# Layer 3 attention scores: bf16 penalties issued ahead of the fp32 score products in some steps

## Chip, cores and metric

The kernel runs on one core of a Trainium2 chip. The metric is the device time of one execution in microseconds (us); lower is better. Before the change the median of three runs is 3193.77 us.

## What is computed

The reference applies four layers to a tensor of 4 images, 256 channels, 48 x 48 points. Each layer is `x = x + conv(groupnorm(x))`. Layers 0 to 2 are convolutions. Layer 3, which the change touches, is a linear attention over square windows of three sizes (whole side, half, quarter), eight heads of 32 channels:

```
for w in WINDOWS:                      # 1, 2, 4
    ws = Hh // w
    wk = _box(Ik, ws, Hh, Ww)          # box sums of k over a ws x ws window
    wkv = _box(Ikv, ws, Hh, Ww)        # box sums of k v^T
    attn = jnp.einsum('bdhw,bdfhw->bfhw', q, wkv)
    norm = jnp.einsum('bdhw,bdhw->bhw', q, wk)
    outs.append((attn / (norm[:, None] + 1e-06)).reshape(b, C, Hh, Ww))
o = jnp.concatenate(outs, axis=1)
return jnp.einsum('bchw,oc->bohw', o, Wout) + bout[None, :, None, None]
```

`q` and `k` are sigmoids, so every product of a query with a key is positive.

## The kernel before

Everything runs in one launch. Layers 0 to 2 fill the time up to about 1405 us of the trace; from there to the end layer 3 runs, with the projections of the next image (`proj_ps`) woven in.

Layer 3 doesn't form box sums of `k v^T`. It computes scores, query times key, masks away the keys that a query's window doesn't hold, and multiplies by `v`. The loop goes over 48 blocks: 4 images, 2 groups of four heads (`ct`), 6 bands of eight query rows (`rb`). A block is a list of steps from `steps_of` (L1968). One step makes scores for 128 keys (8 rows by 16 columns) at a time against up to 512 query columns for each of four heads. Each head's scores fill one PSUM bank of 512 fp32; two heads share a tile `s` of two banks, so a step has two tiles, called pair 0 and pair 1 here. The pool `ps_s` holds just these two tiles, so the scores of a step wait until the masking of the step before has read its pair.

There are four kinds of step:

- **near** (`add_half`, L1952): keys of the same band or the next one, two products per head, of 320 and 192 columns, and all three windows. Penalties cover columns 192 to 384, so they cut through both products.
- **packed** (`add_strips`, L1930): keys two bands away. Three products of 128 columns each hold the columns that the widest window sees in part; penalties cover just these 384 columns. `add_middle` puts one product of 112 or 117 columns of the middle window behind them.
- **far** (`add_far`, L1938): keys three bands away, two halves, products of 280 and 168 columns (keys below) or 320 and 192 (keys above). Penalties cover all 448 or 512 columns.
- **middles**: what of the middle window found no room in a packed step; no penalties.

The widest window is masked by **penalties**: a matmul of `picks` (24 rows of each 32-row group, 128 columns, bf16) with columns of `masks` (bf16) adds -1024 where a key isn't seen, and a ReLU in `masked` (L2039) makes these scores zero. The other two windows are masked by a product with a 0/1 mask on DVE, and on POOL for the smallest.

`scores` (L2012) issues, for each product, pair 0's two heads and pair 1's two heads, each head in its own 32-row group of the array. An fp32 matmul becomes two loads of weights and two passes. After all products come the penalties, in the same order of heads. The first product in the bank has `start=True`; later ones write into columns of the bank not yet written, or, like the penalties, add onto what stands there.

The order on every engine is the program's: `pe`, `dve`, `act`, `pool` and `sync` are wrapped in `InOrder`. The main loop at the end of the kernel issues, for position n of the stream, the scores of step n, its masking, then the sums (`acc`, products with `v`, method `sums`, L2146) of step n-2, and lets `advance` issue other jobs (projections, `keys_ps`, `out_ps`, norms) as far as a planned time allows. In steps with parts of the middle window ACT masks pair 1 first and DVE pair 0, then they change places; in far steps ACT takes pair 0 and DVE pair 1.

On PE the scores use the array as 32-row tiles (shown as 32*128 or 24*128), and the work before and after them uses 32-column tiles (128*32) or 32*32. All matmuls are issued through one helper line, so the profile shows L251 for all of them; groups are told apart by the names of the tiles: `s<-qs,ks` are score products, `s<-masks` penalties.

Of the kernel before, what the change touches and what calls it, by code (L numbers as in the profile page):

```python
# [254 lines left out]
def conv_preact_kernel(  # L255
# [1374 lines left out]
    with (  # L1630
# [371 lines left out]
        class Block:  # L2002
# [8 lines left out]

            def scores(self, st):  # L2012
                ss = [ps_s.tile([P, 2, 512], F32, tag="s", name="s") for _ in range(NPR)]
                for a, c, ranges, (r0, r1), at, n in st.products:
                    for pr, s in enumerate(ss):
                        for j in range(2):
                            head = slice((2 * pr + j) * D, (2 * pr + j + 1) * D)
                            pe.matmul(
                                s[:, j, at : at + n],
                                kvs[self.b, self.ct, a][0][head, c, :],  # L2020
                                of_columns(self.qs[head], ranges, r0, r1),
                                start=(at == 0),
                                stop=not st.penalties and at + n == st.columns,
                            )
                for lo, hi, first in st.penalties:
                    for pr, s in enumerate(ss):
                        for j in range(2):
                            g = 2 * pr + j
                            rows = slice(g * D, g * D + RB + KC)
                            pe.matmul(  # L2030
                                s[:, j, lo:hi],
                                picks[rows, :],
                                masks[rows, PEN_AT + first : PEN_AT + first + hi - lo],
                                start=False,
                                stop=True,
                            )
                return ss

            def masked(self, st, ss):  # L2039

# [128 lines left out]
        def of_columns(t, ranges, r0, r1):  # L2169

            (x0, x1), n = ranges[0], len(ranges)
            if n == 1:
                return t[:, x0:x1, r0:r1]
            size, apart = x1 - x0, ranges[1][0] - x0
            assert n == 2 and x0 == 0 and apart % size == 0 and ranges[1][1] == apart + size
            return t.rearrange("p (g x) r -> p g x r", x=size)[
                :, 0 : apart // size + 1 : apart // size, :, r0:r1
            ]
# [191 lines left out]
        for n in range(len(stream) + LAG):  # L2370
            if n < len(stream):
                i, st, at, last = stream[n]
                if at == 0:
                    begun(i)
                ss = blocks[i].scores(st)
# [3 lines left out]
            if n >= LAG:  # L2379
                i, st, at, last = stream[n - LAG]  # L2380
# [64 lines left out]
```

## Time and profile before

| | |
|---|---|
| runs of the kernel before | 3193.77, 3187.84, 3198.49 us; median 3193.77 |
| the profiled execution | 3194.66 us, of which the span of instructions is 3192.8 us |
| mean granted TensorE clock | 0.955 of full speed; 0.98 from 1420 us to the end |
| layer 3's share of the span | about 1405 to 3192.8 us |
| busy in 1420 to 3192 us (1772 us) | PE 1678.7, DVE 1082.9, POOL 1176.5, ACT 712.9 us |
| score products `s<-qs,ks` | 8704 passes, 589.1 us busy |
| penalties `s<-masks` | 1664 matmuls (416 steps of four), 168.3 us busy |
| idle time of `s<-qs,ks` weight loads | 256.2 us in 8704, of which 77.7 us until ACT has released a pair |

PE's records are pipelined: a matmul's duration holds a fixed latency besides the time in which its columns stream, and neighbours overlap. Distances from start to start are what the work takes; durations compare only with durations of the same kind. PEld are the loads of weights; PE can load the next weights while a matmul streams.

### The profile page before, as it was taken

To read this page: it belongs to the slowest core of one execution; us is meant where nothing else is said; L and a number is where in the kernel's file an instruction comes from. 1 tells how busy PE (TensorE), PEld (TensorE's weight loads), DVE (VectorE), ACT (ScalarE), POOL (GpSimd) and SP (SyncE) were. 2 spreads that over 40 slices of the span, in tenths; PEclk is the share of its full clock that TensorE was granted. 3 is DMA by queue.
4 is the path that set the end of the run, shared out by engine and by line. 5 is a ranking of instruction groups with operands and counts; after the bars stand their busy time and mean duration, and the time that the engine had idled before them with its cause. 6 is when DMAs were issued, how large, how long until landed. Compare 5 with 4: busy or idle time off the path is not lost.

```text
span 3192.8 us, 98649 instructions
## 1 busy us (share of the span) xinstructions
PE 2866.5 (90%) x42698; PEld 2024.3 (63%) x42698; DVE 2002.8 (63%) x3779; ACT 994.5 (31%) x1965; POOL 1356.8 (42%) x1915
## 2 busy tenths in 40 slices
PE   3678999898989987889998899898999989999999
PEld 2456868677766856576665556565666655666665
DVE  7976658747855831376776666675546765555454
ACT  0002211121111144325543235553236532333322
POOL 0000012003000312046788877787757687644443
PEclk9788899999999988899999999999999999999999
DMA  8746512431443144324565765564544456411222
GB/s 276 212 161 185 159 62 103 130 123 53 136 123 110 60 127 146 111 79 140 162 200 147 215 187 156 163 192 142 162 138 144 141 157 186 134 40 44 89 76 69
DMA packets 380037, 434.05 MB, mean 136 GB/s; under 512 B 129843, under 2 KB 335443, under 8 KB 378451
## 3 DMA queue, kind: packets, MB, share of 16 engines
q1 hardware_dynamic: 378403, 425.76, 43.3%
q8 instruction: 338, 5.54, 0.8%
q0 software_dynamic: 144, 1.17, 0.2%
q10 hardware_dynamic: 1056, 0.79, 0.1%
q14 instruction: 96, 0.79, 0.1%
HBM read 288.11 MB, written 140.68 MB: 134 GB/s over the span
## 4 chain that ended last, share of the span: by engine, by line
PE 62%; DVE 11%; POOL 4%; DMA 4%; ACT 3%; issue 2%; SPq 2%; ACTq 0%; DVEq 0%; POOLq 0%
PE s L251 16%; PE cv L251 15%; PE acc L251 15%; PE out_ps L251 5%; PE proj_ps L251 5%; PE ap L251 3%; DVE sm L251 2%; DVE l2v L251 2%; SPq L251 2%; POOL sm L251 2%; POOL nhi L251 1%; ACT sm L251 1%; DVE v L251 1%; PE keys_ps L251 1%; DVE x L251 1%
## 5 line engine op out<-in xcount | busy, mean ns | idle before, releaser
L251 DVE TENSOR_TENSOR sm<-s,masks 128x448 f32<-128x448 f32 (+9 forms) x1408 | 619.9, 497 | 437.1 <-PE s L251 379.5
L251 POOL TENSOR_TENSOR sm<-sm,masks 128x704 f32<-128x704 f32 (+11 forms) x512 | 596.5, 1186 | 513.9 <-DVE sm L251 513.5
L251 ACT ACTIVATE sm<-s 128x384 f32<-128x384 f32 (+2 forms) x736 | 441.5, 609 | 746.6 <-PE s L251 589.7
L251 PE MATMUL cv<-vx,wt 128*128 128x288 f32 x2080 | 562.6, 427 | 92.2 <-DVE vx L251 49.9
L251 PE MATMUL s<-qs,ks 32*128 32x320 f32 (+10 forms) x8704 | 589.1, 360 | 34.7 <-ACT sm L251 20.1
L251 PE MATMUL acc<-sm,vs 128*32 128x128 f32 (+19 forms) x18432 | 606.0, 276 | 6.3 <-issue 6.2
L251 PEld LDWEIGHTS acc<-sm,vs 128*32 128x32 f32 x18432 | 443.0, 110 | 190.2 <-issue 143.4
L251 PEld LDWEIGHTS s<-qs,ks 32*128 32x128 f32 x8704 | 395.1, 186 | 256.2 <-issue 112.0
L251 PEld LDWEIGHTS cv<-vx,wt 128*128 128x128 f32 x2080 | 404.5, 199 | 214.6 <-issue 56.8
L251 POOL MEMSET v<- 128x16 f32 (+1 forms) x120 | 18.7, 216 | 765.0 <-DVE vx L251 639.8
L251 PE MATMUL cv<-v,wl 128*128 128x384 f32 x1152 | 226.8, 357 | 27.3 <-DVE x L251 9.4
L251 PEld LDWEIGHTS cv<-v,wl 128*128 128x128 f32 x1152 | 216.7, 197 | 38.4 <-issue 17.9
L251 DVE TENSOR_SCALAR sm<-s 128x896 f32<-128x896 f32 (+1 forms) x96 | 110.9, 1156 | 116.0 <-PE s L251 92.5
L251 PE MATMUL s<-masks 24*128 24x192 bf16 (+3 forms) x1664 | 168.3, 284 | 0.0
L251 POOL TENSOR_TENSOR v<-l2v,v 128x384 fp32r<-128x384 f32 x96 | 108.5, 1160 | 120.4 <-ACT v L251 111.7
L251 PE MATMUL cv<-pad,wl 128*128 128x384 bf16 x864 | 145.5, 331 | 5.1 <-ACT pad L251 5.1
L251 POOL TENSOR_TENSOR nhi<-nhi,nq 128x384 f32<-128x384 f32 x144 | 147.9, 1047 | 0.0
L251 PE MATMUL out_ps<-o,wout_sb 128*32 128x384 f32 x1152 | 122.0, 495 | 6.2 <-ACT ns L251 2.4
L251 PEld LDWEIGHTS <-wl 128*128 128x128 bf16 x864 | 84.5, 98 | 65.5 <-issue 7.9
L251 PE MATMUL out_ps<-stage,wout_sb 128*32 128x384 f32 x1152 | 121.8, 491 | 0.2 <-issue 0.2
L251 DVE TENSOR_TENSOR pt<-cs 128x184 f32<-128x184 f32 x144 | 120.1, 838 | 0.1
L251 PE MATMUL ap<-seen,xT 120*128 120x120 f32 (+3 forms) x832 | 120.1, 304 | 0.0
(175 smaller groups left out, 3419.8 us busy)
## 6 DMA issues: line engine op xcount, KB each, us to landing
wt<-wt SPq DMA_DIRECT2D x48, 768.0 KB
kb_d<-pt SPq DMA_DIRECT2D x48, 576.0 KB
rc<-r_d SPq DMA_DIRECT2D x192, 144.0 KB
nhi<-kb_d SPq DMA_DIRECT2D x120, 192.0 KB
nlo<-kb_d SPq DMA_DIRECT2D x88, 192.0 KB
o_d<-stage SPq DMA_DIRECT2D x24, 576.0 KB
o<-o_d SPq DMA_DIRECT2D x24, 576.0 KB
wl<-wl_d SPq DMA_DIRECT2D x16, 768.0 KB
```

The source lines that it names most:

```text
L251: return lambda *args, **kwargs: self.tc.keep_in_program_order(op(*args, **kwargs))
```

## The change

In steps in which every product lies either wholly inside the penalties' columns or wholly outside, `scores` now calls the penalties first: they open the bank (`start=True`), and the products are added onto them where they overlap. In the other steps the order stays. The penalties' loop moves into a method of its own, `penalise`. The test `ahead_` is true for packed, far and middles steps and false for near ones; middles have no penalties, so nothing is issued differently there.

```
             def scores(self, st):
                 ss = [ps_s.tile([P, 2, 512], F32, tag="s", name="s") for _ in range(NPR)]
-                for a, c, ranges, (r0, r1), at, n in st.products:
+                ahead_ = all(at + n <= st.lo or at >= st.hi or (st.lo <= at and at + n <= st.hi) for *_, at, n in st.products)
+                if ahead_:
+                    self.penalise(st, ss, True)
+                for m, (a, c, ranges, (r0, r1), at, n) in enumerate(st.products):
                     for pr, s in enumerate(ss):
                         for j in range(2):
...
-                                start=(at == 0),
-                                stop=not st.penalties and at + n == st.columns,
+                                start=m == 0 and not (ahead_ and st.penalties),
+                                stop=(ahead_ or not st.penalties) and m == len(st.products) - 1,
                             )
+                if not ahead_:
+                    self.penalise(st, ss, False)
+                return ss
+
+            def penalise(self, st, ss, opening):
+
                 for lo, hi, first in st.penalties:
                     for pr, s in enumerate(ss):
                         for j in range(2):
...
-                                start=False,
-                                stop=True,
+                                start=opening,
+                                stop=not opening,
                             )
-                return ss
```

The number of matmuls, their shapes and operands, the tiles of the array that they use and everything on the other engines stay as they were.

## The prediction

> **What bounds the kernel now.** I read the page's busy times and its chain of work first. The chain is the work that ended last, followed back.
>
> ```profile
> PE 2866.5 (90%) x42698; PEld 2024.3 (63%) x42698; DVE 2002.8 (63%) x3779; ACT 994.5 (31%) x1965; POOL 1356.8 (42%) x1915
> ...
> PE 62%; DVE 11%; POOL 4%; DMA 4%; ACT 3%; issue 2%; SPq 2%; ACTq 0%; DVEq 0%; POOLq 0%
> ```
>
> PE carries the chain. In layer 3 it does so more: asked for 1530 to 3192 us alone, the chain has PE s 29.4%, acc 26.3%, out_ps 10.0%, proj_ps 6.4%, keys_ps and norm_ps 1.5% each, 75% in all. The masking (DVE, POOL and ACT `sm`, 9.4%) stands between one step's scores and the next. A stretch of the chain in order of time (start us, us, what):
>
> ```profile
> 2474.15 0.86 PE proj_ps L251 x16
> 2475.01 1.16 PE s L251 x20
> 2476.17 1.46 PE acc L251 x48
> 2477.64 0.86 PE proj_ps L251 x16
> 2478.50 1.29 PE s L251 x20
> 2479.79 0.87 PE acc L251 x32
> ```
>
> PE goes from scores to sums to filler without a pause; every ns cut from such a piece of `s` moves what follows.
>
> **Which steps change.** The groups by shape, for 1405 to 3192 us, give the penalties by width (shapes, count, busy us, mean ns):
>
> ```profile
> L251 PE MATMUL s<-masks 24*128 24x192 bf16 x1024 | 88.8, 244 | 0.0
> ...
> L251 PE MATMUL s<-masks 24*128 24x384 bf16 x256 | 29.7, 325 | 0.0
> L251 PE MATMUL s<-masks 24*128 24x512 bf16 x192 | 26.6, 376 | 0.0
> ```
>
> Width 192 is the near steps: strips from column 192 to 384 cut both products, so they stay. 384 wide is packed (256/4 = 64 steps), 512 is far with keys above (48), and the rest of the 1664, 192 matmuls of width 448, is far with keys below (48). **160 of 416 steps change.**
>
> **One far step on PE**, timeline of PE from 2399.2 us (start us, us for the union of the row, xcount):
>
> ```profile
> 2399.00 0.51 PE L251 MATMUL proj_ps<-xn,wq_sb 128*32 128x384 f32 x4
> 2399.44 1.04 PE L251 MATMUL s<-qs,ks 32*128 32x168 f32 x16
> 2400.30 0.37 PE L251 MATMUL s<-masks 24*128 24x448 bf16 x4
> 2400.60 0.82 PE L251 MATMUL acc<-sm,vs 128*32 128x280 f32 x12
> ```
>
> An fp32 pass streams two cycles a column at 2.4 GHz, a bf16 one one cycle: here start-to-start distances are 140 ns for 168 columns, 235 for 280. The last of the four proj_ps passes starts at 2399.02 and streams 320 ns to 2399.34; scores start at 2399.44, a drain of 96 ns. Penalties start at 2400.30, stream 187 ns, the last of the four heads starts 20 ns behind the first, and sums start at 2400.60, a drain of 92 ns. From scores to sums: 1.16 us.
>
> Within it, the durations of the first four score passes and of those that follow (min/median/max):
>
> ```profile
> L251 PE MATMUL s<-qs,ks x4: 405/405/405, 2399.4 to 2399.5; 32*128 32x168 f32 x4
> ...
> L251 PE MATMUL s<-qs,ks x11: 301/394/405, 2399.4 to 2399.8; 32*128 32x168 f32 x7, 32*128 32x280 f32 x4
> ```
>
> A 168-column pass takes 301 ns, the first 405: 104 ns more. Its weights are loaded at that very moment (the loads start at 2399.44 too, so they were not pulled ahead across the drain). Later loads lie behind a streaming pass. **A step opens with one exposed load of fp32 weights.** What a load costs is plain where matmuls stream a single column, at 348 us:
>
> ```profile
> 347.78 1.03 PE L251 MATMUL sum_ps<-ones,wl 128*128 128x1 f32 x8
> ...
> 348.67 0.29 PE L251 MATMUL sum_ps<-ones_b,kept 128*128 128x1 bf16 x6
> ```
>
> With single durations of 250 and 163 ns (groups of that stretch), the distance is (1030-250)/7 = 111 ns for fp32 weights and (290-163)/5 = 25 ns for bf16.
>
> **What the Trainium skill says.** "TensorE: Matmul & The Clock Gate", section "LDWEIGHTS (loading the stationary operand)": a load takes its columns over 1.2 GHz, 107 ns for 128, whatever the rows; the trace agrees (104 exposed, 111 apart). Its section "Weight-path perf modes" says that non-fp32 weights of 128 columns load fast, measured at about twice; the trace has 111 against 25 ns, more than four times, and decides. Penalty loads have this width: they last 95 ns in the record against 186 for the score weights. "TensorEngine Tiling (Array Packing)", section "Key Properties": a change of tiling mode drains the array; the trace has 92 to 96 ns. Penalties and scores are both tiled by 32 rows, so their order changes no mode. "PSUM — Partial Sum Buffer", section "The four PSUM rules": the opening matmul clears the bank's bits, later ones add where something was written and overwrite elsewhere; no time hangs on that in any row here.
>
> **The change, part by part.** *Opening with a bf16 load*: the exposed load falls from 107 to 25 ns, -82 ns. *fp32 weights behind the penalties*: 107 ns of load beside 160, 187 or 213 ns of streaming (384, 448, 512 columns), so nothing; if that cover fails, +107. *Penalties at the end*: gone; their weight loads were hidden behind score passes, so only their stream moves. *Exit*: the drain stays; middles steps already leave from an fp32 pass with the same 92 ns. Sum for the far step: before 107 + 2x140 + 2x233 + 187 + 20 + 92 = 1152 (measured 1160), after 25 + 187 + 746 + 20 + 92 = 1070. For the packed step at 2176.86 (penalties 2177.85, sums 2178.12: 1.26 us) the eight passes go at the load's pace, 111 ns: before 107 + 7x111 + 98 + 160 + 20 + 92 = 1254, after 1172. Both -82.
>
> The switch from bf16 to fp32 in one row group is shown nowhere in this tiling. Nearest is the 128*128 tiling of layer 1, where an fp32 product follows a bf16 one:
>
> ```profile
> 736.41 0.33 PE L251 MATMUL cv<-pad,wl 128*128 128x384 bf16 x1
> 736.58 0.65 PE L251 MATMUL cv<-vx,wt 128*128 128x288 f32 x2
> ```
>
> 0.17 us against 160 ns of streaming: load hidden, no drain. I take 0. Bounds: no gain below this, as there is no less work than none; a loss up to a drain of 96 and a reload of 107.
>
> *Waits*: the wait for a pair's release moves from the first product to the penalty. Behind pair 1's penalty now stand all products of pair 0; before, pair 0's first product ran while pair 1 was awaited. This matters in the steps in which PE stalls inside, some 80 of the 160 by their start-to-sums distances (over 60 ns beyond the shortest). There pair 1's row groups end last and set the exit; their own sequence is shorter by the same 82 ns. Pair 0 led by up to its first product, two passes (214 ns packed, 280 to 533 far), and now leads by a penalty (160 to 213). In the worst case, a stalled far step that opens with its wide product, pair 0 ends 533-213-82 = 240 ns later. Its reader is ACT (896 or 1024 elements, about 1.0 us); DVE, which starts later on pair 1 and takes 1.13 to 1.23 us, ends last. So I take 0, and 20 steps x 0.24 = 5 us as the bound. No queue other than PE's changes; DMAs, masks and the planner's costs stay.
>
> **The sum.** 160 x 82 ns = 13.1 us of PE work, all of it in the chain's kind of piece. It reaches the end only where the chain goes through the step. Followed back in the trace, the chain covers 80% of the changed steps' time on PE (PE's 75% plus some of the masking in series with it says the same); elsewhere POOL, a DMA or the queue sets the pace. So 13.1 x 0.8 = 10.5 us. The profiled execution, 3194.66 us (span 3192.8 and 1.9 around it), lies 0.9 above the median of the runs; off the median, 3193.8 - 10.5 = **3183 us**. Next to bind in a shortened step is the same PE queue.
>
> **Rivals.** *A, the forecast*: 3183; with 65 to 100% landing and the scatter of the runs, 3178 to 3188. *B, the gain is mostly absorbed*: score loads waited 77.7 us for ACT's release, half of the changed steps stall, and a later pair 0 costs up to 5 us; with a third of it left, 4 us, 3190. Against it: the masking waits for the scores far longer (DVE idle 379.5, ACT 589.7 us until PE `s`), so most masking starts sooner too. *C, slower*: in a row group the fp32 weights can't load behind a bf16 pass, or the switch drains. Drain and reload, 96 + 107 - 82 = +121 ns a step, x 160 x 0.8 = 15.5 us: 3209. It decides from 82 ns of extra a step. Against it stand the rows at 736 us, and that at 2184.74 us penalties of one pair stream beside products of the other. *That nothing is reordered* is excluded by the columns of far and packed steps.
>
> **Chances.** A 0.70, B 0.22, C 0.08. About 0.3%, 9.6 us, is what this measurement can tell from no change, and A's centre lies just beyond it: I give A 0.78 to pass it, B 0.05. Faster 0.56, slower 0.06 (C past +9.6), same 0.38. The range 3177 to 3192 holds A and most of B.
>
> **What would show it.** Right: far steps 1.08 and packed 1.17 us from start to sums when unstalled; the first row is `s<-masks`, the first fp32 pass with its ordinary duration; `s<-masks` takes over the idle time ahead of scores. C shows as more than 190 ns from a 448-wide penalty to its product. B shows as shorter steps with longer waits of PE for ACT or DVE. Wrong altogether: if the opening bf16 load in this tiling isn't 25 ns.

## The result, and the profile after

Over six runs the changed kernel takes 3169.37 us in the median (3160.70 to 3179.41), the kernel before 3193.52 (3187.84 to 3198.49). The ratio is **0.9932, 95% interval [0.9912, 0.9952]**: 22 us faster, twice what was forecast, and below the range of 3177 to 3192. Run twice more beside other kernels, it gave 0.9945 [0.9927, 0.9963] and 0.9915 [0.9894, 0.9936]. The profiled execution took 3170.42 us, its span 3168.6.

On the page after, the busy times, the chain of work that ended last, and the groups of the two kinds of matmul:

```profile
PE 2838.8 (90%) x42698; PEld 2009.7 (63%) x42698; DVE 2001.7 (63%) x3779; ACT 993.4 (31%) x1965; POOL 1355.0 (43%) x1915
...
PE 63%; DVE 12%; ACT 4%; POOL 3%; DMA 3%; issue 3%; SPq 1%; DVEq 0%; ACTq 0%; POOLq 0%
...
L251 PE MATMUL s<-qs,ks 32*128 32x320 f32 (+10 forms) x8704 | 551.8, 353 | 24.6 <-ACT sm L251 16.5
...
L251 PE MATMUL s<-masks 24*128 24x192 bf16 (+3 forms) x1664 | 171.6, 287 | 12.8 <-ACT sm L251 8.7
```

The counts are those of before; the other engines' busy times moved by 1 to 2 us. PE still bounds the kernel. `s<-qs,ks` went from 589.1 to 551.8 us busy for the same 8704 passes: not less work, but less time in which a pass waited for its weights. `s<-masks` now has idle time ahead of it, since it comes first.

Split by shape, layer 3 of before (after the bar: busy us, mean ns of one; then idle us ahead):

```profile
L251 PE MATMUL s<-qs,ks 32*128 32x128 f32 x1536 | 77.5, 293 | 9.8 <-ACT sm L251 6.0 <-DMA ks<-k_d 2.3 <-DVE sm L251 0.4
...
L251 PE MATMUL s<-qs,ks 32*128 32x168 f32 x384 | 32.9, 332 | 1.9 <-issue 0.9 <-ACT sm L251 0.8
...
L251 PE MATMUL s<-masks 24*128 24x448 bf16 x192 | 23.2, 349 | 0.0
```

and of after:

```profile
L251 PE MATMUL s<-qs,ks 32*128 32x128 f32 x1536 | 60.0, 277 | 0.1
...
L251 PE MATMUL s<-masks 24*128 24x384 bf16 x256 | 32.8, 333 | 9.8 <-ACT sm L251 7.0 <-DVE sm L251 0.5
...
L251 PE MATMUL s<-qs,ks 32*128 32x168 f32 x384 | 23.7, 303 | 0.0
L251 PE MATMUL s<-masks 24*128 24x448 bf16 x192 | 23.2, 359 | 2.2 <-ACT sm L251 1.0
```

The mean 168-column product falls from 332 to 303 ns, which is the duration of a pass whose load is hidden (301). The 448-wide penalty, 349 ns at the end of a step, takes 359 ns at its start: a mere 10 ns for being first, where the product paid 104. The 9.8 us of idle time ahead of packed steps have changed owner and not size.

**An unstalled far step**, the one that the prediction dissected, timeline of PE after:

```profile
2386.06 0.83 PE L251 MATMUL proj_ps<-xn,wq_sb 128*32 128x384 f32 x8
2386.82 0.37 PE L251 MATMUL s<-masks 24*128 24x448 bf16 x4
2387.02 0.93 PE L251 MATMUL s<-qs,ks 32*128 32x168 f32 x16
2387.88 0.68 PE L251 MATMUL acc<-sm,vs 128*32 128x280 f32 x8
```

From start to sums it is 1.06 us where it was 1.16. The single starts, in ns from the first penalty, are 0 (penalty), 200, 347 (168 columns), 488 and on (280 columns), 1057 (sums). (Where this text says how long a matmul streams, that is an estimate from distances: 140 ns for 168 fp32 columns, here and in the prediction, and half of that for a bf16 column, from the 431 ns that two matmuls of 512 add in the dose below.) Over all unstalled changed steps the median difference is **-104 ns** (far and packed alike).

**A stalled packed step**, one in which pair 1 has to wait for its reader. Timeline of before:

```profile
2412.87 0.61 PE L251 MATMUL proj_ps<-wv_sb,xn 128*32 128x256 f32 x8
2412.95 0.59 DVE L251 TENSOR_TENSOR sm<-s,masks 128x432 f32<-128x432 f32 x1
...
2413.41 1.27 PE L251 MATMUL s<-qs,ks 32*128 32x128 f32 x29
...
2414.93 0.40 PE L251 MATMUL acc<-sm,vs 128*32 128x224 f32 x4
```

and the same step after:

```profile
2400.14 0.61 PE L251 MATMUL proj_ps<-wv_sb,xn 128*32 128x256 f32 x8
2400.22 0.59 DVE L251 TENSOR_TENSOR sm<-s,masks 128x432 f32<-128x432 f32 x1
...
2400.69 0.52 PE L251 MATMUL s<-masks 24*128 24x384 bf16 x4
...
2400.88 1.21 PE L251 MATMUL s<-qs,ks 32*128 32x128 f32 x32
...
2402.02 0.40 PE L251 MATMUL acc<-sm,vs 128*32 128x224 f32 x4
```

Work before it, its reader on DVE and its work are the same; scores to sums go from 1.52 to 1.33 us. Over all stalled changed steps the median is **-185 ns**, 80 more than in the unstalled ones. The single starts show where (ns from the first pass of pair 0; the third kernel is an experiment below):

```
                                        before   after   split wait
DVE ends reading pair 1's old scores       124     124      125
pair 1: row that carries the DVE wait      163     177      178
pair 1: first matmul                       270     181      182
pair 1: first matmul of the product        270     357      190
sums start                                1515    1329     1439
```

In before, the row at 163 stands among the weight loads, but it loads nothing: the trace names it `EVENT_SEMAPHORE`. It is an instruction of its own that waits for DVE and takes 51 ns. Only at 239 does the load of the weights follow, carrying a second wait, and at 270 the first pass. **From the reader's end to pair 1's first matmul it is 146 ns before and 57 ns after.** From there to the sums it is 1245 and 1148, -97. The two make the -186 of this step.

The instructions of the trace say what differs. Before, pair 1's first fp32 product needs two waits, one on DVE (the reader) and one on PE's own counter, and one of them stands in an extra instruction. The penalty's load and its matmul carry one each:

```
before   EVENT_SEMAPHORE      [waits DVE]
         LDWEIGHTS s<-qs,ks   [waits PE]
         MATMUL    s<-qs,ks
after    LDWEIGHTS masks      [waits DVE]
         MATMUL    s<-masks   [waits PE]
```

In layer 3 the extra instructions that wait for DVE fell from 358 to 214. That fp32 as such starts late is excluded by other rows of before. From the semaphore's update to the first pass, where that is under 220 ns, it is 136 ns in the median of 127 fp32 products behind an extra instruction, but 44 ns in the median of 170 fp32 products with a single wait, on ACT; of those with a single wait on DVE, 25 take 40 to 49. Bf16 penalties with one wait on the load and one on the matmul take 47 ns (73 in after). (Counted from the reader's end, each is about 10 ns more.)

In sum, 79 unstalled steps x 104 ns and 80 stalled ones x 185 ns are 8.2 + 14.8 = **23.0 us** of PE work (the first step of all, which waits for layer 2, is left out). Near and middles steps have a median of 0. Layer 3, from its first score matmul to the end, took 1781.1 us before and 1781.0 when run again; after, 1759.8, 1764.4 and 1751.3 in the three profiles, 22.6 less on average. The third lost a little less to the throttle: 32 us of clock in layer 3 (time times the share not granted), against 35 to 36 in the other four.

### The profile page after: what moved, and what is told of

It reads as the page before. It is cut to its first block, busy times and chain, and to the rows that moved or that the text cites. A ratio compares the mean times of both kernels' runs of the same rounds, so it can differ in the third digit from the quotient of the medians.

```text
span 3168.6 us, 98361 instructions
## 1 busy us (share of the span) xinstructions
PE 2838.8 (90%) x42698; PEld 2009.7 (63%) x42698; DVE 2001.7 (63%) x3779; ACT 993.4 (31%) x1965; POOL 1355.0 (43%) x1915
## 4 chain that ended last, share of the span: by engine, by line
PE 63%; DVE 12%; ACT 4%; POOL 3%; DMA 3%; issue 3%; SPq 1%; DVEq 0%; ACTq 0%; POOLq 0%
PE s L251 16%; PE cv L251 15%; PE acc L251 15%; PE out_ps L251 5%; PE proj_ps L251 5%; DVE sm L251 3%; PE ap L251 2%; DVE l2v L251 2%; POOL sm L251 1%; ACT sm L251 1%; DVE v L251 1%; POOL nhi L251 1%; SPq L251 1%; PE keys_ps L251 1%; DVE x L251 1%
## 5 line engine op out<-in xcount | busy, mean ns | idle before, releaser
L251 PE MATMUL s<-qs,ks 32*128 32x320 f32 (+10 forms) x8704 | 551.8, 353 | 24.6 <-ACT sm L251 16.5
L251 PEld LDWEIGHTS s<-qs,ks 32*128 32x128 f32 x8704 | 384.0, 186 | 170.6 <-issue 75.3
L251 PEld LDWEIGHTS <-masks 24*128 24x128 bf16 x1664 | 65.7, 92 | 100.0 <-issue 61.0
```

Of the source, the lines that this page charges most:

```text
L251: return lambda *args, **kwargs: self.tc.keep_in_program_order(op(*args, **kwargs))
```

## The experiments

Two theories stood against each other for the part beyond the forecast. **W**: pair 1's first fp32 product starts late because both waits are on it, and any bf16 matmul ahead of it that takes one of them over mends this. **L**: all of it comes from the opening load, and stalled steps merely show it twice, once for each pair. All ratios are to the kernel before, on the same chip.

**The split wait alone.** The order stays that of before. In the 160 steps a bf16 matmul of one column goes ahead of pair 1's first product, which writes over it:

```
+    def touch(self, s, pr, j, n):
+        g = 2 * pr + j
+        rows = slice(g * D, g * D + RB + KC)
+        pe.matmul(s[:, j, 0:n], picks[rows, :], masks[rows, PEN_AT : PEN_AT + n],
+                  start=True, stop=True)
...
+    if m == 0 and pr == 1 and j == 0 and (far or packed):
+        self.touch(s, pr, j, 1)
     pe.matmul(s[:, j, at : at + n], ...)
```

> The order of before (products, then penalties). In far and packed steps one bf16 matmul of a single column, whose value the product behind it overwrites, is put ahead of pair 1's first product, so that the two waits of that product are split over its load and its pass. Theory W (an fp32 product that waits for two semaphores starts 146 ns after the reader of its bank ends, a bf16 load and pass with one wait each 57 ns after): pair 1 starts some 89 ns sooner in the 80 stalled steps, unstalled steps lose 0 to 10 ns, so 5 to 7 us less than before, about 3187. Theory L (all of the gain is the opening load and its cover): nothing gained, 3193 to 3195.

Measured 0.9944 [0.9924, 0.9964]; again:

> The first experiment once more, because its 0.9944 of before is more than its own steps show (80 stalled steps 76 ns shorter, unstalled ones 14 ns longer: 5 us, 9 us with what else moved in that trace). If the step times tell all: 4 to 9 us less than before, 0.997 to 0.999. If splitting the wait does something more that the steps do not show: 0.994 again, as far below before as the changed kernel of the same call.

0.9938 [0.9920, 0.9955]. The stalled step from above:

```profile
2402.34 0.59 DVE L251 TENSOR_TENSOR sm<-s,masks 128x432 f32<-128x432 f32 x1
...
2402.81 0.38 PE L251 MATMUL s<-qs,ks 32*128 32x128 f32 x2
2402.99 0.17 PE L251 MATMUL s<-masks 24*128 24x1 bf16 x1
...
2403.00 1.04 PE L251 MATMUL s<-qs,ks 32*128 32x128 f32 x28
...
2404.25 0.59 PE L251 MATMUL acc<-sm,vs 128*32 128x224 f32 x8
```

Pair 1's product now starts beside the one-column matmul, 65 ns after the reader's end where it was 146. Stalled steps are 77 ns shorter in the median, unstalled ones 14 longer (the extra matmul). That is W: 77 of the 80 ns that stalled steps gained beyond the others come with one column of bf16 and no reordering at all. But the whole kernel gains more (18 to 20 us) than these steps, which sum to -8.8 and -9.1 us in the two profiles. That is taken up below.

**The opening without cover.** The order of before again, but all four heads' banks are opened by one-column bf16 matmuls, so that a bf16 load comes first and nothing streams over the fp32 load:

```
+    if far or packed:
+        for pr, s in enumerate(ss):
+            for j in range(2):
+                self.touch(s, pr, j, 1)
     for a, c, ranges, (r0, r1), at, n in st.products:
```

> The order of before. In far and packed steps each head's bank is first touched by a bf16 matmul of one column, whose value the product behind it overwrites: the step opens with bf16 loads, but nothing streams that could cover the fp32 load behind. If cover is what makes the 104 ns: unstalled steps 5 to 25 ns longer than before, stalled ones 60 to 80 ns shorter by the split waits, about 5 us less than before. If opening in bf16 were enough by itself: 104 and 185 ns as in the changed kernel, 21 us less.

Measured 0.9976 [0.9962, 0.9990]. Unstalled steps +11 ns, stalled -65. The far step, timeline and then durations of its first rows (min/median/max):

```profile
2386.34 0.18 PE L251 MATMUL s<-masks 24*128 24x1 bf16 x4
2386.38 1.01 PE L251 MATMUL s<-qs,ks 32*128 32x168 f32 x16
```

```profile
L251 PE MATMUL s<-qs,ks x4: 384/384/388, 2386.4 to 2386.4; 32*128 32x168 f32 x4
```

The first fp32 passes last 384 ns and not 301: their load is exposed although bf16 came first. So the -104 need the **cover**, 160 to 213 ns of penalty streaming over a 104-ns load, as the prediction had it. What the opening alone gives is the split wait again, 76 ns between stalled and unstalled. This kernel splits the same waits as the first experiment (here too 214 extra instructions wait for DVE), yet as a whole it gains 8 us and not 18 to 20.

**Far steps alone**, the test `ahead_` limited to them, packed steps as before:

> The change in far steps alone; packed steps keep their order. By the step times of the two traces (unstalled 104 ns, stalled 185 ns less): 55 x 104 + 41 x 185 ns = 13.3 us, of which 93% land by the stage's length: 12.4 us, about 3181. If the packed steps carry more than their share, as the longer stalls in front of them could make it, less: 7 to 10 us.

Measured 0.9943 [0.9925, 0.9961]. Far steps -104 and -184, packed steps 0: the parts don't act on one another. 55 x 104 + 41 x 184 are 13.3 us; layer 3 took 18.2 less, with 4 us less lost to the throttle than in the profile of before.

**A dose.** What does a microsecond in these steps cost at the end? The changed kernel, and two more bf16 matmuls of 512 columns for each head at the start of each of the 160 steps, written over afterwards:

```
+    if ahead_ and st.penalties:
+        for _ in range(2):
+            for pr, s in enumerate(ss):
+                for j in range(2):
+                    self.touch(s, pr, j, 512)
     if ahead_:
         self.penalise(st, ss, True)
```

> The changed kernel with added work: in each of the 160 steps two bf16 matmuls of 512 columns per head ahead of the penalties, whose values the penalties overwrite. That is 2 x 213 ns = 0.43 us a step, 69 us in all. It measures what share of a change in these steps reaches the end: with 93%, 64 us over the changed kernel, 3233; with the 80% of the prediction, 55 us, 3224.

Measured 1.0107 [1.0087, 1.0127]. Each step is 431 ns longer (two streams of 213), stalled or not; against the changed kernel's trace the changed steps sum to +69.6 us. Layer 3 took 1809.8 us, 50.0 more than after: **72% lands**. By the runs it is more: 1.0107 against 0.9931, the mean of the changed kernel's three ratios, is 56 us or 81%. The forecast's 0.8 lies within what this can tell, and it is not what failed.

**The split wait in the other steps.** The changed kernel, and the one-column matmul ahead of pair 1's first product in near and middles steps:

```
+    if m == 0 and pr == 1 and j == 0 and not (far or packed):
+        self.touch(s, pr, j, 1)
```

> The changed kernel, and in near and middles steps, whose order it leaves alone, the same single-column bf16 matmul ahead of pair 1's first product. Theory W: 134 stalled steps of these kinds start pair 1 some 89 ns sooner, about 11 us, of which 9 to 10 land: about 3159. Theory L: as the changed kernel, 3168 to 3171.

Measured 0.9903 [0.9885, 0.9921]; again:

> The changed kernel with the split wait in near and middles steps once more, beside the changed kernel on the same chip. By step times (99 stalled near steps 71 ns shorter, 155 unstalled ones 14 ns longer, middles even): 3 to 5 us below the changed kernel. If the 0.9903 of the first time is real beside it: 8 to 12 us below.

0.9890 [0.9870, 0.9909]. Near steps that stall are 71 to 74 ns shorter, those that don't 14 longer. It is the fastest of all: 3155.13 and 3158.63 us.

**Near steps opened by a penalty as well.** The changed kernel; in near steps a penalty of 192 columns covers the 192-column product whole and opens, the other strip's 128 columns follow at the end (128 columns more a head than before):

```
+    if not ahead_:
+        self.penalise(st, ss, True, [st.opener])
...
+    self.opener = (left[c] + x0 * RB, left[c] + x1 * RB, PENALTY_AT[0, "open", half][0])
+    self.penalties.append((..., PENALTY_AT[0, "rest", half][0]))
```

> The changed kernel, and near steps opened as well: the 192-column product goes first and is covered whole by a 192-column penalty with zeros where nothing is masked, which opens the bank; the other strip's 128 columns of penalty stay at the end. 128 more bf16 columns stream (53 ns) and 27 ns of the fp32 load stay uncovered: unstalled near steps 104 - 53 - 27 = 24 ns shorter (155), stalled ones 105 ns (99), 14 us, of which 80% land: 11 us below the changed kernel, about 0.9898 of before. If near steps lie off the chain: as the changed kernel, 0.9932 of before.

Measured 0.9931 [0.9911, 0.9952]. Near steps -16 ns unstalled, -89 stalled: again some 73 between the two. 128 more columns are 53 ns of streaming, so -51 would follow from the -104. Most of the other 35 ns is fp32 load left bare, as was expected: a penalty of 192 columns streams 80 ns against a load of 104, and the first pass behind it lasts 350 ns where later ones of its width last 321. Some 6 ns stay unexplained. Beside it on the same chip the changed kernel itself ran again:

> The changed kernel once more, on the chip of the other runs of this call, so that they can be set beside it: 0.9932 of before, within the interval 0.9912 to 0.9952.

It gave 0.9945 [0.9927, 0.9963]; the 4 us between the two can't be told apart.

**Why does the split wait give more than its own steps show?** Three more runs bear on this: the changed kernel a third time, the kernel before against itself, and the split wait in every step on the order of before.

> The changed kernel beside the two others of this call: 0.993 to 0.9945 of before.

> The kernel before against itself, for a second profile of it and to see what the comparison makes of no change: ratio 0.998 to 1.002 with an interval that holds 1. The first profile had its third layer 1781 us long. If it was an ordinary one: 1778 to 1784 again, and split waits (1763 to 1765) do more than their steps show. If it was a long one: 1772 to 1777, and step times tell most of it.

> The order of before with the split wait in every step, near and middles too. By step times: 10 us in far and packed steps, 7.4 - 2.1 us in near steps, nothing in middles: 15 us, 12 to 15 landing, about 0.9955 of before. If a split wait gives twice what its steps show, as the first and eighth run did (0.9944, 0.9938): 28 to 32 us, about 0.9905.

Measured 0.9915 [0.9894, 0.9936], 1.0000 [0.9989, 1.0011] and 0.9939 [0.9917, 0.9962]. Before against itself leaves room for a bias of 0.1% at most. The split wait in all steps gave no more than in the 160, though near steps that stall are 65 ns shorter in it; its 160 steps sum to -5.3 us and its near steps to -3.7. So the effects don't add up one by one: the split wait alone takes off about 19 us, the change, which holds the same split waits, 22, and the change with split waits in near and middles steps 33. With the 8 us of the run without cover, split waits as such are not what is worth 19.

One thing that differs is pauses of PE that the profile puts down to no semaphore (`issue`). The longest, and the next wait behind it, in before:

```profile
2577.44 0.42 PE L251 MATMUL acc<-sm,vs 128*32 128x280 f32 x1
2580.72 1.44 PE L251 MATMUL acc<-sm,vs 128*32 128x280 f32 x12 [2.86 <-issue]
...
2584.89 1.34 PE L251 MATMUL s<-qs,ks 32*128 32x192 f32 x14 [1.17 <-ACT sm L251]
```

and the same place with the split wait:

```profile
2564.56 0.96 PE L251 MATMUL acc<-sm,vs 128*32 128x280 f32 x16
2565.34 0.82 PE L251 MATMUL norm_ps<-nhi,head_sel 128*32 128x384 f32 x6
2569.28 2.56 PE L251 MATMUL s<-qs,ks 32*128 32x192 f32 x16 [3.12 <-ACT sm L251]
```

The pause stands in both profiles of before and in neither of the split wait, but most of it isn't gained: PE waits longer for ACT just behind. In layer 3 such pauses of over 150 ns sum to 12.2 and 10.8 us in before, 6.9 and 5.8 with the split wait, and 9.6, 8.4 and 5.7 after.

What PE waits for there can be read from the DMA packets. The page of before lists a queue of instructions:

```profile
q8 instruction: 338, 5.54, 0.8%
```

12 of the 14 pauses in before end 1.2 to 1.6 us after a packet of this queue has landed, and so do 12 of 14 after; of all passes of PE only a tenth start 1.1 to 1.7 us after one. The other two, of 404 and 787 ns, stand in every profile alike. So in most pauses PE seems to wait for its next instructions, and where such a wait falls moves with any change of the instruction stream. This rests on the times alone; no run tests it. How much of the split wait's surplus is due to the pauses, 5 us less of them in all, **stays open**, and so does the rest.

## Why the prediction was wrong, point by point

- *What bounds the kernel*: right. PE leads the chain with 63%, and a dose of work in these steps reaches the end at 72 to 81%.
- *160 of 416 steps change, the rest stay*: right; near and middles steps have a median difference of 0.
- *Opening with a bf16 load, -82 ns*: right in mechanism, mis-sized. Measured **-104**. The bf16 load was put at 25 ns, the distance between 128*128 matmuls of one column. Here the penalty's pass starts 4 ns after its load, and its record is 8 to 10 ns longer than at the end of a step: about 12 ns stay exposed (an estimate from these figures), so -95. Another -10 are in no step of the sum: the four heads start 3.3 ns apart in a step that a bf16 load opens and 6.7 in one that an fp32 load opens, and the last one sets the exit. The 20 ns of that stagger had been kept for both kernels.
- *fp32 weights behind the penalties, 0*: right. The product starts 200 ns after its penalty, 187 of streaming and 13. The run without cover shows its other side. The Trainium skill, "TensorE: Matmul & The Clock Gate", section "The mechanism", says in a list that loads overlap with running matmuls only where the row group differs; ahead of the list it also allows a background buffer for weights. Here the fp32 load starts 9 ns after the penalty's pass in the same row group and is hidden, which fits the second of these and contradicts the first; the measurement decides.
- *Drains*: right for far steps, and nearly for packed ones. Entry 97 to 99 ns (96 before), exit 90 from far steps (92), 101 to 107 from packed ones, which now end on an fp32 product of 112 or 117 columns. The reason given doesn't hold: middles steps leave not after 92 but after 110 to 132 ns, counted from the estimated end of streaming.
- *The switch from bf16 to fp32, 0*, and with it **rival C**: right to set aside, though its sign was drawn too tightly: "more than 190 ns" came out as 200, which is streaming and the 13 ns above. No drain of 96 and no reload of 107 is in it.
- *Waits: "So I take 0"*: **this step failed.** It had pair 1's sequence shorter "by the same 82 ns", and priced the move of the wait only as a possible loss, up to 5 us. It counted how long the wait lasts and what is queued behind it. It didn't count **how the waiting instruction starts once released**: with two waits on one fp32 product, and so an extra instruction, 146 ns, with a wait each on load and matmul 57. The extra instruction at +39 stood in the trace of before, in the stalled steps. Half of the steps are such, so 80 x 81 = 6.5 us were left out.
- *The sum*: 13.1 us of PE work forecast, 23.0 measured: 160 x 22 ns = 3.5 from the opening, 6.5 from the waits. At the forecast's 0.8 this is 18.4, and 3175 us; the ratio puts the kernel at 3172. The shorter pauses, 3 to 4 us on average, would fill the difference, but that isn't shown.
- *Rival B, absorbed*: its sign was shorter steps with longer waits of PE for ACT or DVE. In layer 3 of before PE waited ahead of scores (us in all, times, longest)

```profile
PE s L251 <- ACT sm L251: 20.1, 44, 1.9
...
PE s L251 <- DVE sm L251: 4.7, 11, 1.2
```

and after

```profile
PE s L251 <- ACT sm L251: 25.1, 48, 2.5
...
PE s L251 <- DVE sm L251: 4.2, 10, 0.7
```

4.5 us more, of 23 that were saved: a part was absorbed, not most. Whether pair 0 became late, which was priced with up to 5 us, no run tests by itself.
- *The range*: its low end let all of the 13.1 us land and the runs scatter, but it held no case in which the sum itself was too small. The bound of each unknown cost was drawn on the side of a loss.

## What to carry to other kernels

After a change of tiling mode, put a bf16 matmul that has to be done anyway first into the bank: its load costs about 12 ns there, and the fp32 load behind it vanished where it streamed for longer than that load's 104 ns; with 80 ns of streaming about 29 ns of the load stayed. Where an extra instruction for a second wait stands ahead of a stalled fp32 matmul, let something that carries one wait on its load and one on its matmul, bf16 in these runs, stand there first: one column of it was worth 77 ns in each step that stalled and cost 14 in each that didn't. And price a wait with what follows its release, read from the reader's end to the first matmul in the trace, and not only with its length.

## What had not been expected of the hardware

- An fp32 matmul with two waits has an instruction `EVENT_SEMAPHORE` of 51 ns ahead of it, which starts 39 ns after the reader's end; the load starts at 115 and the first pass at 146. A bf16 load with one wait starts after 53 and its matmul, with the other, after 57. An fp32 matmul with one wait starts as soon as the bf16 one (44 against 47 ns from the semaphore's update).
- The matmul that opens a step sets how far its four heads start apart: 3.3 ns behind a bf16 load, 6.7 behind an fp32 one, and the matmuls of the other type behind it keep that distance. The Trainium skill, "TensorE: Matmul & The Clock Gate", section "Measured speedup vs the span model", states about 4 ns for a tile, which fits the steps opened in bf16 alone.
- Right after a change of tiling mode a bf16 load costs next to nothing: the penalty starts 4 ns after a load whose record lasts 91.
- PE pauses for up to 3 us with no semaphore behind it, most often until 1.2 to 1.6 us after a packet of instructions has landed. These pauses differ by several us between kernels that do nearly the same.
